# Single tiles of a gather fetched row by row: from SyncE alone to SyncE and ScalarE

## The chip, the cores and the metric

The kernel runs on one core of one Trainium2 chip. Times are device microseconds of that core. One execution was also taken by the hardware profiler; its time and its trace are what the profile below shows. The engines are called PE (TensorE), DVE (VectorE), ACT (ScalarE), POOL (GpSimd) and SP (SyncE).

## The reference

A graph layer with attention over all edges. There are 12500 nodes with 64 features and 412500 edges, sorted by receiver (`dst`), with 32 features each.

```
h   = relu(layernorm(x))
msg_in     = [h[src], h[dst], edge]                      # 64 + 64 + 32 per edge
messages   = silu(msg_in @ W1 + b1) @ W2 + b2
att_logits = silu(msg_in @ Wa1 + ba1) @ Wa2 + ba2
att        = softmax(att_logits, over all edges)
aggregated = segment_sum(messages * att, dst)            # per node
out = x + silu([h, aggregated] @ Wu1 + bu1) @ Wu2 + bu2
```

## The kernel before

First, per node, two tables are computed and stored in memory: `ts_d` (what a sender contributes to `msg_in @ [Wa1, W1]`, 128 floats, 512 bytes a row) and `tr_d` (the same for a receiver, with the bias). Then `one_pass` goes over the edges.

Edges come in tiles of 128 (one edge per partition), T = 3224 tiles; K = 8 tiles make a group, so there are NG = 403 groups. For each group the kernel needs the 128 x 8 sender rows. `load(g)` gets them: for each tile GpSimd issues one indirect DMA (line 487) that gathers 128 rows of `ts_d` into `gs`, a buffer from a pool of eight. The receivers of a group are few and lie close together, so their rows come as a window: SyncE loads it with two DMAs (line 506, `wins`, three buffers), and every fourth group it loads edge features and receiver numbers (lines 496 and 499, `eo` and `db`). DVE makes a one-hot matrix from the receiver numbers (line 513), and PE multiplies it and the edge features with the window (line 517) into `pe`.

`begin(g)` adds `pe` to the gathered rows (line 523) and ACT takes the tanh of it (line 526). `end(g)` makes messages and logits on DVE (lines 536 to 547). Groups are put in batches of four for a running softmax: two Exp on ACT (lines 575 and 578) once per batch. `by_node` and the parts of `sum_up` weigh the messages, sum them by node on PE (line 594), copy the sum on ACT (`out_of`, line 600), project it (line 605) and add it to the node sums on DVE (lines 618 to 624).

The main loop is software-pipelined: at iteration g it runs `begin(g)`, then `load(g + 2)`, then `end(g)`, with the summing of an older group in between. Compute instructions are pinned to the order in which they are written. DMAs, register loads and indirect DMAs are not pinned: the scheduler places them on their engine's queue, in the order of its own model, and each engine then runs its queue strictly in order. Every DMA of SyncE and ScalarE counts on one of eight semaphores, given out in turn, and waits until the DMA that had the same semaphore before has landed.

In some groups one tile of the eight is not gathered by GpSimd. This is the subject here. `QUEUES` lists who fetches such single tiles: `(engine, every, phase, n_rows)`. Before, it holds one entry: SyncE, one group in 11, 12 rows in each group. `numbers(q, g)` loads the 128 sender numbers of the tile into `one_src` (line 438). Then `rows(q, g)`, called once per group, loads the next 12 numbers into registers (line 460, one register load from memory) and issues 12 DMAs of one row of 512 bytes each (line 464) into the tile `one_gs`, kept in `alone`. After 11 groups all 128 rows are issued, the group's `load` then gathers 7 tiles only, and `begin` adds the single tile by an instruction of its own (line 525). SyncE's `rows` is called in `load`, behind the window's DMAs.

Of the kernel before, what the change touches and what calls it, by code (L numbers as in the profile page):

```python
# [49 lines left out]
ENG = mybir.EngineType  # L50
# [19 lines left out]
NC = 8  # L70
TABLES = 4

QUEUES = [(ENG.SP, 11, 0, 12)]
EPS = 1e-5
NEG = -3.0e38
BIG = 3.0e38
# [9 lines left out]
def gnn_kernel(ctx: ExitStack, tc: tile.TileContext, n_edges, x, src, src_row, dst, dst_row, first, edge,  # L86
# [70 lines left out]
    with tc.tile_pool(name="node1", bufs=1) as node1, \  # L157
# [132 lines left out]
        for c, nn in chunks:  # L290
            tr = node.tile([P, CB, C], F32, name="tr")[:, :nn, :]
            for b in range(0, nn, 4):
                n = min(4, nn - b)
                pn = node_ps.tile([P, 4, C], F32, name="pn", bufs=4)
                for i in range(0, n, 2):
# [7 lines left out]
        pin(nc.scalar.dma_start(hT_d, hT))  # L303

    one_pass(tc, n_edges, locals())
    again = nc.values_load(wrong[0:1, 0:1], min_val=0, max_val=1,
                           skip_runtime_bounds_check_because="it is the outcome of a comparison")
# [57 lines left out]
def one_pass(tc, n_edges, v):  # L365
# [17 lines left out]
    with ExitStack() as ctx:  # L383
# [25 lines left out]
        for w in wins:  # L409
            nc.vector.memset(w, 0.0)  # L410
            for r in range(2):
                rows = slice(WR + r * DE, WR + (r + 1) * DE)
                nc.vector.tensor_copy(w[rows, :, r, :], we[rows, None, :].to_broadcast([DE, 2, C]))
        with tc.tile_pool(name="work2", bufs=2) as work2, \
# [18 lines left out]
            def numbers(q, g):  # L433

                if g < NG - 4:
                    t = g * K + K - 1
                    rows_at[q, g] = small.tile([1, P], I32, name=f"one_src{q}", bufs=2)
                    nc.sync.dma_start(rows_at[q, g], v["src_row"][:, t * P:(t + 1) * P])

            def rows(q, g):  # L440
                engine, every, phase, n_rows = QUEUES[q]
                if g == 0:
                    numbers(q, phase + every)
                if g < phase:
                    return
                at = (g - phase) % every
                g = g - at + every
                if at == 0:
                    rows_at.pop((q, g - every), None)
                    if (q, g) in rows_at:  # L450
                        alone[g] = work2.tile([P, C], F32, name=f"one_gs{q}")
                if at == every // 2:
                    numbers(q, g + every)
                if (q, g) not in rows_at:
                    return
                a = at * n_rows
                n = min(n_rows, P - a)
                if n <= 0:
                    return
                load, regs = nc.values_load_multi_w_load_instructions(  # L460
                    rows_at[q, g][0:1, a:a + n], engines=[engine], min_val=0, max_val=NP - 1,
                    skip_runtime_bounds_check_because=WHY)
                for k in range(n):
                    dma[engine].dma_start(alone[g][a + k:a + k + 1, :], ts_d[bass.ds(regs[k], 1), :])
# [15 lines left out]
            def load(g):  # L480
# [24 lines left out]
                for r in range(2):  # L505
                    nc.sync.dma_start(win[r * R:(r + 1) * R, :, r, :],
                                      tr_w[bass.ds(at_sp[g], R), :, :])
                for q in range(len(QUEUES)):
                    if QUEUES[q][0] == ENG.SP:
                        rows(q, g)  # L510
# [9 lines left out]
            def begin(g):  # L520

                n = K - (g in alone)
                pin(nc.vector.tensor_tensor(gss[g][:, :n, :], pes[g][:, :n, :], gss[g][:, :n, :], ALU.add))  # L523
                if n < K:
                    pin(nc.vector.tensor_tensor(gss[g][:, n, :], pes[g][:, n, :], alone.pop(g), ALU.add))
                pin(nc.scalar.activation(pes[g], gss[g], AF.Tanh))  # L526

            def end(g):

                s = batch[g]  # L530
                if g == starts[s]:
                    lgs[s] = small.tile([P, B * K], F32, name="lg")
                gs, th = gss.pop(g), pes.pop(g)

                def message():
                    pin(nc.vector.scalar_tensor_tensor(acts[g % ACTS][:, :, 0:U], th[:, :, U:C], 1.0,  # L536
                                                       gs[:, :, U:C], op0=ALU.add, op1=ALU.mult))

                if g < NG - 1:
                    message()  # L540
                att = th[:, :, 0:U]
                pin(nc.vector.scalar_tensor_tensor(att, th[:, :, 0:U], 1.0, gs[:, :, 0:U],  # L542
                                                   op0=ALU.add, op1=ALU.mult))
                pin(nc.vector.tensor_tensor(att, att, wa2[:, None, :].to_broadcast([P, K, U]),  # L544
                                            ALU.mult))
                k = (g - starts[s]) * K
                pin(nc.vector.tensor_reduce(lgs[s][:, k:k + K], att, AX.X, ALU.add))  # L547
                if g == starts[s] + size[s] - 1:
                    mts[s] = top(s)
                if g == NG - 1:  # L550
                    message()
# [108 lines left out]
            for g in range(NG):  # L660
# [3 lines left out]
                if more and g == NG - 1:  # L664
                    next(more)
                begin(g)
                if more and g < NG - 1:
                    next(more)
# [368 lines left out]
```

## Time and profile before

| what | value |
|---|---|
| median of 2 runs | 6256.53 us (6245.09 to 6267.97) |
| the profiled execution's own time | 4115.52 us |
| its span, first to last instruction | 4113.8 us |
| mean granted TensorE clock in it | 0.633 |
| gathers by GpSimd (line 487) | 3188, 3018.7 us busy |
| rows by SyncE (line 464) | 4608 of 0.5 KB |
| mean busy share of the DMA engines, 1000 to 4050 us | 0.36 to 0.38 |
| waits of ACT before the tanh (line 526) | 2585.7 us |

The span and the engine shares belong to the profiled execution, which took less than the two timed ones. Busy time does not hold register, branch, semaphore and DMA-issuing instructions. So SyncE and the issuing part of ScalarE have no share in the page's first part; they are seen in the timeline as "SPq" and "ACTq". A group's line gives busy time, the mean duration in ns, and behind the bar the idle time of the engine before such instructions with what ended most of it. "issue" there means that the engine waited for nothing that the profile shows.

### The profile page before, as it was taken

Reading aid. Unit: us, or ns where it says so; the run is one execution under the profiler, and the core shown is the slowest. Engines: PE = TensorE matmul, PEld = TensorE weight load, DVE = VectorE, ACT = ScalarE, POOL = GpSimd, SP = SyncE. Lnnn points to the kernel's source line nnn. Section 1 sums busy time; section 2 is a strip of 40 time slices with the busy share of each in tenths; the row PEclk is TensorE's granted clock in tenths of the full one; section 3 lists DMA queues with packets and bytes.
Section 4 is the critical chain, followed back from the end, with each engine's and each line's share of the span. In section 5 each row is a group of like instructions: output and inputs, shape, how many; then the busy total and the mean of one; then the engine's idle time right before and its main releaser. Section 6 shows DMA issues by size and latency. Waiting matters only on the chain.

```text
span 4113.8 us, 59789 instructions
## 1 busy us (share of the span) xinstructions
PE 2284.8 (56%) x10980; PEld 1852.9 (45%) x10980; DVE 3021.4 (73%) x8518; ACT 584.3 (14%) x1235; POOL 3035.8 (74%) x3213
## 2 busy tenths in 40 slices
PE   5555545555556555556555555555555555555555
PEld 4444434444445444444444444444444444444444
DVE  6777867777777777777777777777777777777777
ACT  3211111111111111111111111111111111111112
POOL 3777777777777777777777777777777777777773
PEclk8666666666565666665566666666666556566665
DMA  7344443443434333333333333333333333333334
GB/s 270 88 102 101 99 105 92 105 101 97 102 93 99 86 91 84 88 91 81 91 84 89 91 81 91 83 89 91 81 91 82 91 91 81 92 81 90 91 78 112
DMA packets 220602, 393.50 MB, mean 96 GB/s; under 512 B 77077, under 2 KB 146554, under 8 KB 207034
## 3 DMA queue, kind: packets, MB, share of 16 engines
q0 software_dynamic: 102016, 209.13, 20.8%
q1 hardware_dynamic: 116826, 170.81, 17.0%
q10 hardware_dynamic: 1376, 9.67, 0.6%
q14 instruction: 294, 2.41, 0.2%
q8 instruction: 90, 1.47, 0.2%
HBM read 363.58 MB, written 25.72 MB: 95 GB/s over the span
## 4 chain that ended last, share of the span: by engine, by line


## 5 line engine op out<-in xcount | busy, mean ns | idle before, releaser
L487 POOL DMA_INDIRECT gs<-ts_d,src_sb x3188 | 3018.7, 947 | 1022.1 <-issue 952.1
L517 PE MATMUL pe<-wins,eo 128*128 128x256 f32 x3224 | 1477.3, 638 | 967.7 <-DVE eo L513 819.6
L517 PEld LDWEIGHTS pe<-wins,eo 128*128 128x128 f32 x3224 | 1000.5, 325 | 1265.8 <-DVE eo L513 970.2
L523 DVE TENSOR_TENSOR gs<-pe,gs 128x1024 f32<-128x1024 f32 (+1 forms) x403 | 487.7, 1211 | 775.5 <-DMA gs<-ts_d,src_sb 740.0
L526 ACT ACTIVATE pe<-gs 128x1024 f32<-128x1024 f32 x403 | 413.8, 1027 | 2585.7 <-DVE gs L523 1997.7
L588 DVE TENSOR_SCALAR wt<-iota_w,dloc,p 128x40 f32<-128x40 f32 x3224 | 734.0, 320 | 0.1
L594 PE MATMUL sp<-wt,acts 128*65 128x40 f32 x6448 | 608.9, 267 | 0.7 <-DVE wt L588 0.7
L594 PEld LDWEIGHTS sp<-wt,acts 128*65 128x65 f32 x6448 | 578.7, 183 | 1.0 <-DVE wt L588 0.8
L605 PEld LDWEIGHTS mt<-ss,w2u 65*128 65x128 f32 x806 | 224.8, 293 | 371.3 <-issue 321.5
L513 DVE TENSOR_SCALAR eo<-db,bj 64x256 f32<-64x256 int32 x806 | 259.7, 360 | 158.6 <-DMA db<-in_dst_row_dram 151.5
L564 PE MATMUL mt<-ident,mx 128*128 128x128 f32 x103 | 45.1, 437 | 547.3 <-DVE sums L622 538.2
L605 PE MATMUL mt<-ss,w2u 65*128 65x40 f32 x806 | 184.9, 324 | 261.4 <-DVE gm L571 257.9
L542 DVE SCALAR_TENSOR_TENSOR pe<-pe,gs 128x512 f32<-128x512 f32 x403 | 281.3, 698 | 13.0
L544 DVE TENSOR_TENSOR pe<-pe,w_all 128x512 f32<-128x512 f32 x403 | 281.4, 698 | 12.8
L536 DVE SCALAR_TENSOR_TENSOR acts<-pe,gs 128x512 f32<-128x512 f32 x403 | 278.2, 690 | 15.7 <-ACT pe L526 4.0
L547 DVE TENSOR_REDUCE lg<-pe 128x8 f32<-128x512 f32 x403 | 278.4, 691 | 13.7
L564 PEld LDWEIGHTS mt<-ident,mx 128*128 128x128 f32 x103 | 18.4, 179 | 557.7 <-issue 556.0
L624 DVE COPY stand<-nmax 64x40 f32 x806 | 163.4, 203 | 0.6
L622 DVE TENSOR_TENSOR sums<-sums,mt 64x40 f32 x600 | 113.2, 189 | 15.0 <-PE mt L605 10.9
L575 ACT ACTIVATE scale<-fall 128x1 f32<-128x1 f32 x103 | 20.9, 203 | 645.1 <-DVE fall L574 629.2
L600 ACT COPY ss<-sp 65x40 f32<-65x40 f32 x403 | 73.5, 182 | 20.7 <-PE sp L594 20.3
L618 DVE SCALAR_TENSOR_TENSOR sums<-sums,scale,mt 64x40 f32 x206 | 51.6, 251 | 11.4 <-PE mt L605 7.3
(92 smaller groups left out, 577.7 us busy)
## 6 DMA issues: line engine op xcount, KB each, us to landing
one_gs<-ts_d SPq DMA_DIRECT2D x4608, 0.5 KB
eo<-in_edge_dram SPq DMA_DIRECT2D x100, 512.0 KB
db<-in_dst_row_dram SPq DMA_DIRECT2D x200, 256.0 KB
gs<-ts_d,src_sb POOLq DMA_INDIRECT x3188
wins<-tr_d SPq DMA_DIRECT2D x806, 32.0 KB
ts_d<-ts SPq DMA_DIRECT2D x5, 896.0 KB
tr_d<-tr ACTq DMA_DIRECT2D x5, 896.0 KB
hT_d<-hT ACTq DMA_DIRECT2D x1, 3136.0 KB
```

The lines of the kernel that those rows point to most:

```text
L487: nc.gpsimd.indirect_dma_start(out=gs[:, j, :], out_offset=None, in_=ts_d[:, :], in_offset=bass.IndirectOffsetOnAxis(ap=src_sb[:, t + j:t ...
L513: pin(nc.vector.tensor_scalar(eo[:WR, e], db[:, e], bj[:, g, h:h + 1], None, op0=ALU.is_equal))
L517: pin(nc.tensor.matmul(pe[:, 2 * q:2 * q + 2, :], eo[:, q * P:(q + 1) * P], win[:, q // 2, :, :], start=True, stop=True))
L523: pin(nc.vector.tensor_tensor(gss[g][:, :n, :], pes[g][:, :n, :], gss[g][:, :n, :], ALU.add))
L526: pin(nc.scalar.activation(pes[g], gss[g], AF.Tanh))
L536: pin(nc.vector.scalar_tensor_tensor(acts[g % ACTS][:, :, 0:U], th[:, :, U:C], 1.0, gs[:, :, U:C], op0=ALU.add, op1=ALU.mult))
L542: pin(nc.vector.scalar_tensor_tensor(att, th[:, :, 0:U], 1.0, gs[:, :, 0:U], op0=ALU.add, op1=ALU.mult))
L544: pin(nc.vector.tensor_tensor(att, att, wa2[:, None, :].to_broadcast([P, K, U]), ALU.mult))
L547: pin(nc.vector.tensor_reduce(lgs[s][:, k:k + K], att, AX.X, ALU.add))
L588: pin(nc.vector.tensor_scalar(wt[:, j, :], iota_w[:, j // H, :], dloc[:, g * K + j:g * K + j + 1], p[:, k + j:k + j + 1], op0=ALU.is_equal ...
L594: pin(nc.tensor.matmul(sp, acts[g % ACTS][:, j, :], wt[:, j, :], start=j == 0, stop=j == K - 1))
L605: pin(nc.tensor.matmul(pp, w2u.rearrange("s h u -> s (h u)"), sps.pop(g), start=True, stop=True))
```

## The change

There are now two entries in `QUEUES`. SyncE fetches a single tile for one group in twelve, 12 rows per group. ScalarE fetches one for one group in sixteen, starting two groups later, 8 rows per group; its rows are issued by a call in `begin`, written behind the tanh. The row numbers of both are loaded by SyncE.

```diff
-QUEUES = [(ENG.SP, 11, 0, 12)]
+QUEUES = [(ENG.SP, 12, 0, 12), (ENG.Activation, 16, 2, 8)]
@@ in begin(g)
                 if n < K:
                     pin(nc.vector.tensor_tensor(gss[g][:, n, :], pes[g][:, n, :], alone.pop(g), ALU.add))
                 pin(nc.scalar.activation(pes[g], gss[g], AF.Tanh))
+                for q in range(len(QUEUES)):
+                    if QUEUES[q][0] == ENG.Activation:
+                        rows(q, g)
```

The functions that this uses are unchanged:

```python
def rows(q, g):
    engine, every, phase, n_rows = QUEUES[q]
    ...
    at = (g - phase) % every
    g = g - at + every          # the group whose single tile is being fetched
    ...
    a = at * n_rows
    n = min(n_rows, P - a)
    ...
    load, regs = nc.values_load_multi_w_load_instructions(
        rows_at[q, g][0:1, a:a + n], engines=[engine], ...)
    for k in range(n):
        dma[engine].dma_start(alone[g][a + k:a + k + 1, :], ts_d[bass.ds(regs[k], 1), :])
```

## The prediction

> **What bounds the kernel now.** I read the page first: engine shares, then the costliest groups. Columns of the first line are busy time, share of the span and instruction count; of the group lines, count, busy us and mean ns, then the idle time before the group and what ended it.
>
> ```profile
> span 4113.8 us, 59789 instructions
> PE 2284.8 (56%) x10980; PEld 1852.9 (45%) x10980; DVE 3021.4 (73%) x8518; ACT 584.3 (14%) x1235; POOL 3035.8 (74%) x3213
> ...
> L487 POOL DMA_INDIRECT gs<-ts_d,src_sb x3188 | 3018.7, 947 | 1022.1 <-issue 952.1
> ...
> L523 DVE TENSOR_TENSOR gs<-pe,gs 128x1024 f32<-128x1024 f32 (+1 forms) x403 | 487.7, 1211 | 775.5 <-DMA gs<-ts_d,src_sb 740.0
> L526 ACT ACTIVATE pe<-gs 128x1024 f32<-128x1024 f32 x403 | 413.8, 1027 | 2585.7 <-DVE gs L523 1997.7
> ```
>
> VectorE (73%) and GpSimd (74%) look equal, but their idle time differs. VectorE waits for something real, 740 us for gathers. GpSimd's idle ended on "issue": it waited for nothing. So a gather costs its 947 ns plus a gap that always follows it. The timeline, second and third columns start and length, shows this beat, with what SyncE and ScalarE do beside it:
>
> ```profile
> 2014.12 0.86 SPq L506 DMA_DIRECT2D wins<-tr_d  x2
> 2014.21 0.94 POOL L487 DMA_INDIRECT gs<-ts_d,src_sb  x1 [0.30 <-issue]
> ...
> 2015.46 0.94 POOL L487 DMA_INDIRECT gs<-ts_d,src_sb  x1 [0.30 <-issue]
> ...
> 2015.91 1.22 DVE L523 TENSOR_TENSOR gs<-pe,gs 128x1024 f32<-128x1024 f32 x1 [0.21 <-issue]
> ...
> 2016.15 4.82 SPq L464 DMA_DIRECT2D one_gs<-ts_d  x12
> 2016.71 0.94 POOL L487 DMA_INDIRECT gs<-ts_d,src_sb  x1 [0.30 <-issue]
> ...
> 2017.17 1.03 ACT L526 ACTIVATE pe<-gs 128x1024 f32<-128x1024 f32 x1 [0.93 <-DVE gs L523]
> ```
>
> Gathers start every 1.25 us (2014.21, 2015.46, 2016.71), whatever VectorE does. GpSimd's whole timeline runs so from 50.42 to 4042.24: 3188 gathers x 1.25 = 3985 us of those 3992. The group beat is 8 x 1.25 = 10.0 us. VectorE needs 3021.4/403 = 7.5 us a group, PE 5.7. The waits of SyncE's queue tell that it too has room; its long waits are for buffers that PE frees:
>
> ```profile
> SPq L506 <- PE pe L517: 291.7, 69, 9.9
> SPq L506 <- PE mt L605: 256.1, 138, 10.8
> SPq L506 <- PE sp L594: 99.0, 84, 5.2
> ```
>
> So in the profiled execution GpSimd's count of gathers sets the time. The chain section is empty and cannot confirm it.
>
> The profiled execution took 4115.52 us (span plus 1.7), the median of the two runs shown is 6256.53: 2141 us more, a factor of 1.520. No view shows where these lie. A step may carry over unchanged, or stretched by 1.520; I keep both ends.
>
> **What the Trainium skill says.** "DMA: Bandwidth & Descriptors", section "Issuing engines are not separate DMA queues": DMAs from different engines run on the same 16 DMA engines, and several issuers save only issue time. That is the question here: rows are issued beside GpSimd, and it is GpSimd's issue time that binds. The DMA engines have room, mean share 0.36 to 0.40 in the windows of the loop. The section "Latency and other measured facts" of that page gives a register load from memory a floor of about 600 ns; the trace has 527 at least and a median of 933 ns for line 460, and I use the trace. "SBUF — State Buffer", section "SBUF: two separate sides", warns that VectorE in its two-port modes keeps GpSimd from writing descriptors. The trace disagrees for this execution: gathers last 940 to 944 ns from minimum to median. In the longer runs it could be what adds time, which no view decides; then a gather costs more and removing one saves more.
>
> **The change part by part.**
>
> Singles before: one in 11 groups, 11 to 396, makes 36 (4608 rows / 128). After: SyncE's groups 12 to 396 step 12 are 33, ScalarE's 18 to 386 step 16 are 24; 12a = 16b + 2 has no solution, so none coincide. 57 singles: 21 gathers fewer, 3167, and the changed program's order holds 3167.
>
> Gathers: 21 x 1.25 = -26.2 us, all on the path. Stretched by 1.520: -39.9.
>
> SyncE: 33 x 128 = 4224 rows, 384 fewer. A burst of 12 takes 4.82 us, 0.40 each: -154 us; 33 x 11 = 363 instead of 396 register loads, -33 x 0.93 = -31 us; 21 more loads of row numbers, x 0.29 (10.4 us busy over 36 in the trace) = +6. About -180 us, off the path: SyncE waits for PE anyway. Counted 0.
>
> ScalarE: 24 x 128 = 3072 issues and 24 x 16 = 384 register loads. ScalarE issued only big DMAs in the trace, so a row's cost there is not shown. The nearest row is SyncE's 0.40 us: 3072 x 0.40 + 384 x 0.93 = 1229 + 357 = 1586 us, or 8 x 0.40 + 0.93 = 4.1 us in a group. Beside its 584 us that is 53% of the span. It lies in the 2585.7 us that ScalarE idles before line 526. Tanh takes 1.03 us, starts right after the add and leaves 10.0 - 1.1 = 8.9 us; the row work fits twice. Low bound 0; high bound: its cover gone, what exceeds 8.9 us in a group goes to VectorE. Taken: 0.
>
> How late may tanh be? In the timeline the add at 2008.05 ends at 2009.28, tanh at 2010.34, and the first user (line 536) starts at 2012.23: 1.9 us free. Beyond it VectorE has 10.0 - 7.5 = 2.5 us a group. Behind those stand eight gather buffers, so that GpSimd may run several groups ahead while VectorE catches up. This matters because the rows aren't spread evenly. In the changed program's order 173 of 403 intervals between tanhs hold none, and about 30 hold 24 to 33. Thirty-two rows are 32 x 0.40 + 4 x 0.93 = 16.5 us, 7.6 over the 8.9. VectorE regains that in three groups at 2.5. Counted 0.
>
> VectorE: 21 groups more split the add, 128 x 128 apart in 0.28 us (36 x 272 to 281 ns), while the rest of the add shrinks by an eighth. Under 21 x 0.28 = 6 us, beside waits for gathers. 0.
>
> DMAs: a row moved to ScalarE or left with a gather moves the same 512 bytes. 0.
>
> Sum: 4115.5 - 26.2 = 4089.3 us against the profiled execution. Onto the median: 6256.5 - 26.2 = 6230.3 unchanged, 6256.5 - 39.9 = 6216.6 stretched. I take the middle, 6223 us, -0.5%.
>
> **The rivals.**
>
> Slower: the two queues lock each other. In both programs every DMA of SyncE or ScalarE waits for the landing of the one eight places earlier, over eight semaphores that both queues now share in turn. Of 3072 ScalarE rows, 1301 wait on a DMA of SyncE; 1000 SyncE rows and 210 window loads (line 506) wait on a row of ScalarE. ScalarE stands at tanh until the add; SyncE can then go no more than eight DMAs further, and the window for the matmul of line 517 stands behind. If SyncE thereby loses its lead and works only after tanh, a group is: 1.25 add + 1.03 tanh + SyncE's 11 rows x 0.40 = 4.4, register load 0.93, two windows 0.87, a quarter of eo and db (1.5/4 = 0.4) + two landings across queues. A landing is about 1.5 us after issue for window loads (median 1.47 from the trace's landing records). Sum 11.9 us. It decides from 10.0 on: 1.9 x 384 groups = +730 us at most. I put half of it in the rival, since SyncE keeps some lead in the intervals without rows: +365 us. The rival's time: 6256.5 - 26 + 365 = 6595 us. For it: the waits and the bunching are in the order. Against: SyncE's own work falls by 180 us, and buffers give all sides groups of lead. With all of it, 6960.
>
> Faster: SyncE sets the pace of the longer runs. Less the 122 us before the first and after the last gather their group beat would be 6135/403 = 15.2 us, with about 15 DMAs of SyncE, 1.0 us each. Taking 384 of about 5900 away (section 6 of the page, summed) gives -6.5%, 6135 x 0.065 = 399: 5858 us. For it: the unexplained 2141 us. Against: 0.40 us a row in the trace, and SyncE's waits for PE.
>
> No gain: the gathers go, but VectorE or the late tanhs eat the 26 us: 6256 us.
>
> That the change doesn't do what it says is excluded by the 3167 gathers in the order.
>
> **How the numbers follow.** Forecast 0.55, no gain 0.07, locked queues 0.28, SyncE's relief 0.10. Two per cent is 125 us, about what a measurement of this kernel can tell from no change. Forecast and no gain lie within it, and 0.01 of the locked case where it is mild: same 0.63, slower 0.27, faster 0.10. Own range of the forecast: 6170 to 6280 (two-run spread of 0.4% around 6217 to 6230). The range must add 0.2 from the sides: up over the mild and middle locked cases to 6600, down to 6120, which leaves out the relief and the worst lock.
>
> **What would show it.** Right: gathers still every 1.25 us, 3167 of them, ending near 4016 instead of 4042; span near 4088; line 464 on ScalarE at 0.4 us a row; VectorE's waits before line 523 still for gathers. Locked queues: gaps over 0.30 us before gathers, waits of VectorE at line 536 on tanh or of PE at line 517 on wins, and SyncE's waits on PE gone over to its row DMAs. Wrong altogether: a span unchanged while the timed runs move by over 2%; then what binds those is not in the profile.

## The result and the profile after

The change made the kernel slower: 6480.8 us against 6256.5 us (two runs each), ratio 1.038 (1.034 to 1.042). One thing must be known to read any number here: the kernel before takes 6245 to 6394 us on some chips and 4114 to 4123 us on others, and by its time its profile above is of the second kind, while the result is of the first. Ratios below are always to the kernel before on the same chip.

The page of the changed kernel, engine shares and groups:

```profile
span 6482.8 us, 68399 instructions
PE 2277.8 (35%) x10980; PEld 1859.6 (29%) x10980; DVE 3011.0 (46%) x8539; ACT 608.5 (9%) x1235; POOL 3012.3 (46%) x3192
...
L487 POOL DMA_INDIRECT gs<-ts_d,src_sb x3167 | 2995.1, 946 | 3357.4 <-issue 3213.6
L517 PE MATMUL pe<-wins,eo 128*128 128x256 f32 x3224 | 1457.7, 631 | 3228.3 <-DMA wins<-tr_d 1762.1
...
L526 ACT ACTIVATE pe<-gs 128x1024 f32<-128x1024 f32 x403 | 413.7, 1027 | 1384.5 <-DMA one_gs<-ts_d 504.0
```

The gathers are the 3167 foreseen and last 946 ns as before, but GpSimd now idles 3357 us, although the line still says "issue". It does wait: GpSimd's semaphore instructions ahead of the gathers last 10.1 us at the median, where all took at most 43 ns in the kernel before. (Three numbers are the shortest, median and longest duration in ns; first the changed kernel, then the kernel before from its profile above.)

```profile
L487 POOLq EVENT_SEMAPHORE  x399: 17/10132/32252, 47.1 to 6341.2; - x200
```

```profile
L487 POOLq EVENT_SEMAPHORE  x399: 17/43/43, 47.3 to 4026.2; - x200
```

All engines are busy under half of the time. A lower clock is not the reason: the mean granted one fell from 0.633 to 0.589, but PE's busy time is 2277.8 us against 2284.8. Nor are slower transfers: by section 3 of the pages the packets of the gathers took 12.9% of 6482.8 us, 836 us, against 20.8% of 4113.8 us, 856 us. The longest wait of PE's matmuls has become the window of receiver rows (1762 us, `wins`), a DMA of SyncE. So look at SyncE's instructions, in the same two profiles:

```profile
L464 SPq MOVE one_gs<-ts_d x4224: 2/29/1409, 140.8 to 6330.4; - x192
...
L464 ACTq MOVE one_gs<-ts_d x3072: 2/29/1395, 132.7 to 6010.4; - x192
```

```profile
L464 SPq MOVE one_gs<-ts_d x4608: 29/29/38, 89.5 to 3937.1; - x192
```

A move into a register, 29 ns at the median, lasts up to 1409 ns. Instruction by instruction the trace shows spells, mostly of 5 to 25 us, in which each instruction of SyncE, whatever it is, comes about 0.70 us after the one before (or 1.40). Counted from the instruction records, such spells fill some 2700 to 3300 of the 6483 us; the sum depends on how the pauses inside a spell are counted. The profile on which the prediction rests has no slow move at all. A piece of the timeline shows what one does:

```profile
2004.93 15.08 SPq L464 DMA_DIRECT2D one_gs<-ts_d  x8
...
2008.96 0.62 PE L608 MATMUL mt<-ss,w2u 65*128 65x40 f32 x2 [6.59 <-DVE gm L574]
...
2009.38 1.96 PE L597 MATMUL sp<-wt,acts 128*65 128x40 f32 x16
...
2019.84 0.19 DVE L625 TENSOR_TENSOR sums<-sums,mt 64x40 f32 x1 [9.20 <-remote]
...
2020.06 0.19 ACT L603 COPY ss<-sp 65x40 f32<-65x40 f32 x1 [10.31 <-remote]
...
2020.26 0.86 SPq L506 DMA_DIRECT2D wins<-tr_d  x2
...
2025.10 0.94 POOL L487 DMA_INDIRECT gs<-ts_d,src_sb  x1 [7.49 <-issue]
```

Eight rows take SyncE 15.08 us, 1.9 us each instead of 0.40, and the window load behind the rows goes out only at 2020.26. A second thing is late. DVE's addition of line 625 and ScalarE's copy of line 603 need what PE's matmuls of lines 608 and 597 made, which by the trace were over at 2009.58 and 2011.34; both start at 2020. "remote" says that a semaphore rose just before, but that no instruction which raises it had just ended. The semaphore is PE's: it is recorded to rise at 2007.76 and then at 2019.82. So the signal that PE is done comes some 10 us late, in the same spell. GpSimd uses up its buffers and stops 7.49 us. Lastly, the waits of SyncE's queue, in us, number and longest:

```profile
SPq L464 <- DMA one_gs<-ts_d: 190.3, 214, 7.6
SPq L506 <- DMA one_gs<-ts_d: 169.1, 50, 13.9
SPq L499 <- DMA one_gs<-ts_d: 119.9, 42, 6.0
```

SyncE now waits 479 us for rows to land, through the semaphores that the two queues share. Its waits for PE, which led this list before, are nearly gone in the loop: it has lost its lead.

### The profile page after: what moved, and what is told of

Read it like the earlier page. It is cut to its first block, busy times and chain, and to the rows that moved or that the text cites. A ratio compares the mean times of both kernels' runs of the same rounds, so it can differ in the third digit from the quotient of the medians.

```text
span 6482.8 us, 68399 instructions
## 1 busy us (share of the span) xinstructions
PE 2277.8 (35%) x10980; PEld 1859.6 (29%) x10980; DVE 3011.0 (46%) x8539; ACT 608.5 (9%) x1235; POOL 3012.3 (46%) x3192
## 3 DMA queue, kind: packets, MB, share of 16 engines
q0 software_dynamic: 101344, 207.76, 12.9%
## 4 chain that ended last, share of the span: by engine, by line
## 5 line engine op out<-in xcount | busy, mean ns | idle before, releaser
L517 PE MATMUL pe<-wins,eo 128*128 128x256 f32 x3224 | 1457.7, 631 | 3228.3 <-DMA wins<-tr_d 1762.1
L591 DVE TENSOR_SCALAR wt<-iota_w,dloc,p 128x40 f32<-128x40 f32 x3224 | 715.4, 307 | 0.1
L574 DVE TENSOR_REDUCE gm<-mt 128x1 f32<-128x128 f32 x103 | 29.2, 284 | 401.6 <-remote 401.5
```

The costliest lines, as they stand in the source:

```text
L517: pin(nc.tensor.matmul(pe[:, 2 * q:2 * q + 2, :], eo[:, q * P:(q + 1) * P], win[:, q // 2, :, :], start=True, stop=True))
L591: pin(nc.vector.tensor_scalar(wt[:, j, :], iota_w[:, j // H, :], dloc[:, g * K + j:g * K + j + 1], p[:, k + j:k + j + 1], op0=ALU.is_equal ...
```

## The experiments

My theory after the result (the "starved queue"): on some chips SyncE and ScalarE run slowly in spells, and time goes with what stands on their queues. Its rival, from the record: the two queues lock each other by the shared semaphores.

### The kernel before, and each part of the change alone

The kernel before, with its trace:

> The kernel before, unchanged, with its trace. Starved queue (my new theory): in the profile of the changed kernel SyncE has spells in which each of its instructions, even a register move that else takes 29 ns, lasts 0.70 us; they fill about 3285 of 6483 us. The profiled execution of before had none and took 4115 us. If the two timed runs of before (6245 and 6268 us) had them, this trace shows them for about 2900 to 3200 us, gathers interrupted, and a time near 6256. Locked queues (the rival on record): no such spells here, since only SyncE issues rows; a time near 4115, or 6256 with another cause.

No single tiles:

```diff
-QUEUES = [(ENG.SP, 12, 0, 12), (ENG.Activation, 16, 2, 8)]
+QUEUES = []
```

> No single tiles at all: all 3224 tiles are gathered by GpSimd, SyncE issues some 1300 DMAs instead of 5900. Starved queue: SyncE has about 13,800 instructions fewer (three for each of 4608 rows), spells vanish or shrink to a few per cent, GpSimd binds again: 122 + 3224 x 1.25 = 4150 us, ratio 0.66 to the 6256 us of before. If GpSimd's gathers bound the timed runs at 1.9 us each (my prediction's stretched case): 36 more gathers, about 6325 us, ratio 1.01. Locked queues: 4150 to 6325, it says nothing on this one.

SyncE's part alone:

```diff
-QUEUES = [(ENG.SP, 12, 0, 12), (ENG.Activation, 16, 2, 8)]
+QUEUES = [(ENG.SP, 12, 0, 12)]
```

> SyncE's part of the change alone: one group in twelve on SyncE, nothing on ScalarE; 3191 gathers, 4224 rows. Starved queue: SyncE has 384 x 3 + 33 instructions fewer of 17,900, 6.6%; ratio about 0.94 to before, 5880 us. GpSimd bound, stretched: +3 gathers x 1.9 = 6 us, ratio 1.00. Locked queues: as before, 1.00, the loss is then all in ScalarE's part.

ScalarE's part alone:

```diff
-QUEUES = [(ENG.SP, 12, 0, 12), (ENG.Activation, 16, 2, 8)]
+QUEUES = [(ENG.Activation, 16, 2, 8)]
+                if engine == ENG.Activation:
+                    for one in load if isinstance(load, (list, tuple)) else [load]:
+                        pin(one)
                 for k in range(n):
-                    dma[engine].dma_start(...)
+                    row = dma[engine].dma_start(...)
+                    if engine == ENG.Activation:
+                        pin(row)
```

> ScalarE's part of the change alone: one group in sixteen on ScalarE, 8 rows a group, none on SyncE, with ScalarE's row DMAs and register loads kept in written order behind the tanh; 3200 gathers, 3072 rows. Starved queue: if the spells come with the number of instructions of a queue, ScalarE now has 9,600 more and would have spells, but fewer than SyncE had: 4400 to 5400 us, ratio 0.70 to 0.86. If they come with SyncE only: 4120 us, 0.66. Locked queues: SyncE has few DMAs left, so little to lock: near 1.00 of before or what GpSimd allows.

| kernel (kernel before 6394 us) | gathers | rows by SyncE, by ScalarE | us | ratio (95%) |
|---|---|---|---|---|
| before again | 3188 | 4608, 0 | 6404 (one run) | - |
| no single tiles | 3224 | 0, 0 | 5718 | 0.894 (0.891 to 0.897) |
| SyncE's part | 3191 | 4224, 0 | 6219 | 0.973 (0.969 to 0.977) |
| ScalarE's part | 3200 | 0, 3072 | 5810 | 0.909 (0.905 to 0.912) |

The first trace settles where the 2141 us that I could not place lie. The kernel before at 6402 us has the spells, and the profiled execution at 4114 us has not:

```profile
span 6402.2 us, 59789 instructions
...
L464 SPq MOVE one_gs<-ts_d x4608: 2/29/1410, 148.6 to 6258.8; - x192
```

On such a chip a row is not cheap but dear: with 36 more gathers the kernel without rows is 10.6% faster than the one before, where GpSimd's count would make it slower. The size I expected, 4150 us, was missed: spells remain. Without rows SyncE has 3618 instructions left, and now others stand still:

```profile
ACT ss L603 <- remote: 2777.1, 158, 24.2
PEld mt L608 <- ACT ss L603: 2169.8, 115, 23.1
```

ScalarE's short copy (line 603) waits up to 24.2 us, and PE waits for it. It is again PE's signal that is late. In this trace 135 of the 403 copies start more than 3 us after the last matmul of line 597 before them had ended, with ScalarE idle, and in 130 of these a rise of PE's semaphore is recorded in the 0.15 us before the start; the first profile of the kernel before has no such copy. So the spells don't only slow instructions on a queue, as my theory says: signals between engines come late too. SyncE's part alone gives 0.973 where 0.94 was expected of the number of instructions. ScalarE's alone is a miss: 5810 us, where 4400 to 5400 (0.70 to 0.86) was expected. Nor does the time simply go with the number of rows: on this chip the first 384 rows taken from SyncE gave 175 us, the other 4224 only 500 us.

When do the spells come? From the four traces of that chip I took GpSimd's runs of gathers (starts under 2.5 us apart) and the register instructions of SyncE. In the kernel before 1594 of them lasted over 600 ns. 1379 lie inside a run, most of them after its first 5 us, and the other 215 within 6 us after its end. Later than 6 us after a run there are over 3200 register instructions of normal length (under 60 ns) and no slow one; in a run's first 5 us 241 are slow and 2252 normal, between 10 and 20 us 611 and 211. So the spells go with uninterrupted gathering and end soon after GpSimd pauses. GpSimd pauses when its eight buffers are full, and they are emptied by the engines that the spell holds up. That is a correlation in the traces; what starves the queues is not shown. Uninterrupted gathering alone doesn't do it: in the first profile of the kernel before all 3188 gathers are one such run, without a slow register instruction.

### Rows from fixed addresses, and fewer gather buffers

Two experiments were to change the spells: the same DMAs with fewer instructions, and shorter runs of gathers.

```diff
-                    dma[engine].dma_start(alone[g][a + k:a + k + 1, :], ts_d[bass.ds(regs[k], 1), :])
+                    dma[engine].dma_start(alone[g][a + k:a + k + 1, :], ts_d[a + k:a + k + 1, :])
```

> The kernel before with the row DMAs reading fixed rows instead of those named by registers: the same 4608 DMAs of 512 bytes, but the register load and the two register instructions ahead of each DMA are gone. It leaves out the right choice of rows. Starved queue, by instructions: SyncE loses 9600 of its 17,900 instructions, two thirds of what the rows cost (676 us over the kernel without rows): near 5940 us, ratio 0.93. By DMAs: the rows cost what they did, ratio 1.00.

```diff
-    gather = ctx.enter_context(tc.tile_pool(name="gather", bufs=8))
+    gather = ctx.enter_context(tc.tile_pool(name="gather", bufs=4))      # none_b4; 3 in none_b3
```

> No single tiles and four gather buffers instead of eight, so that GpSimd can run ahead by less. In the traces all slow register instructions of SyncE lie in runs of gathers without a break or within 4 us after one, nearly all after its first 5 us; without single tiles a run is 24 gathers at the median, and GpSimd then pauses for a buffer. If the run length drives the spells: shorter runs, fewer stalls, faster than the kernel without single tiles, 5000 to 5500 us. If GpSimd's lead hides the stalls: fewer buffers expose them, slower than 5718.

> The same with three gather buffers, the fewest that the order of the loop allows. A run can hardly pass 8 to 16 gathers. If the run length drives the spells: at or under the time with four buffers. If the lead hides the stalls, or gathers are now exposed behind the end of a group (10 us of gathers + 2 us of landing against three groups): slower, 5900 or more.

Beside them ran the changed kernel with ScalarE's rows in written order (the edit of ScalarE's part, with both entries of `QUEUES`):

> The changed kernel with ScalarE's register loads and row DMAs kept in written order, so that 8 rows stand behind each tanh instead of 0 to 33. Starved queues alone (spells of slow instructions while gathers run, each part costing by itself): the parts measured so far add up, none + 500 us for SyncE's rows + 92 us for ScalarE's = 6310 us, ratio 0.987 to before. Locked queues (shared semaphores tie the two queues, worse where rows are bunched): SyncE still waits hundreds of us for ScalarE's rows; if the bunching makes the lock, 0.99; if the sharing itself makes it, 1.02 to 1.04 as the changed kernel.

They ran on a chip without spells, kernel before 4114 us. Fixed rows 1.0005 (0.9996 to 1.0013): SyncE has 8684 instructions instead of 17,902, and that is worth nothing there. Four buffers without single tiles 1.013 (1.011 to 1.015), three 1.025 (1.023 to 1.026). Rows in written order 0.998 (0.998 to 0.999). What they were meant to tell of the spells they cannot.

### The changed kernel on a chip without spells

> The changed kernel again, beside the kernel before on the same chip. The chips differ: on one the kernel before took 6394 us with spells of slow instructions, on another 4114 us without. Without spells: GpSimd bound says 4114 - 26 = 4088 us, ratio 0.994; locked queues with bunched rows say slower than the version with rows in written order (4107 us, 0.998), 4115 to 4600, ratio 1.00 to 1.12. With spells: 1.038 as measured.

> The changed kernel with ScalarE's rows in written order, 8 behind each tanh, again. Without spells: 0.998 as measured. With spells: if bunching makes the loss, the parts add up, 0.987; if the shared semaphores do, whatever the order, 1.02 to 1.04.

> The kernel before with rows from fixed addresses (it leaves out the right choice of rows), 9600 instructions of SyncE fewer, the same DMAs. Without spells 1.0005 as measured. With spells: if they cost by instructions, 0.93; if by DMAs, 1.00.

> No single tiles and four gather buffers. Without spells 1.013 as measured (eight buffers would give 3224 gathers x 1.25 = 1.009). With spells: if the length of GpSimd's runs drives them, under 0.894, what eight buffers gave; if the lead hides the stalls, over it.

Kernel before 4115 us. Changed kernel 1.013 (1.011 to 1.015), with rows in written order 0.9985 (0.998 to 0.999), fixed rows 1.000, four buffers without single tiles 1.0125. The four once more, on another chip:

> The changed kernel with ScalarE's rows in written order, beside the changed kernel. On a chip without spells 0.998 to 0.999 as measured twice. On a chip with spells: if bunching alone makes the loss, the parts measured there add up, 0.987; if the shared semaphores make it in any order, as the changed kernel, 1.02 to 1.04.

> The changed kernel again. Without spells 1.013 as measured; with spells 1.038 as measured.

> The kernel before with rows from fixed addresses (it leaves out the right choice of rows). Without spells 1.000. With spells: by instructions 0.93, by DMAs 1.00.

> No single tiles and four gather buffers. Without spells 1.013. With spells: under 0.894 if the length of GpSimd's runs drives them, over 0.894 if its lead hides the stalls.

This chip has no spells either (kernel before 4123 us): 0.998, 1.012, 1.000 and 1.013.

So the change loses even where no instruction is slow: +51 us where -26 was forecast. And it is the order of ScalarE's rows that makes the loss, since keeping them in written order takes it away. (The traces show what the order does: between two tanhs stand 8 rows in 382 of 402 cases; as scheduled, none in 173 and 24 to 33 in 27.) The windows of the trace show where. Columns: window, its length, busy us with counts for PE, PE's loads, DVE, ACT and GpSimd, then clock, DMA share and GB/s. First the kernel before, then the changed one, then the one in written order:

```profile
620.00:1320.00 700.00, 404.57 (x1932) 321.53 (x1931) 528.16 (x1508) 99.16 (x214) 529.89 (x559) 0.63 0.40 99
1320.00:2020.00 700.00, 385.17 (x1856) 314.32 (x1856) 511.27 (x1460) 90.49 (x196) 529.19 (x561) 0.62 0.37 88
```

```profile
620.00:1320.00 700.00, 360.61 (x1720) 281.54 (x1721) 474.38 (x1358) 92.85 (x194) 478.68 (x505) 0.62 0.36 91
1320.00:2020.00 700.00, 379.86 (x1941) 316.76 (x1941) 534.34 (x1532) 97.62 (x204) 528.12 (x559) 0.64 0.36 88
```

```profile
620.00:1320.00 700.00, 384.83 (x1802) 292.95 (x1802) 497.53 (x1427) 98.82 (x204) 522.56 (x552) 0.63 0.39 97
```

Behind 1320 us GpSimd issues 559 gathers in 700 us, its full beat. Between 620 and 1320 it is 505: 54 fewer than before, x 1.25 = 67 us. All its nine gaps of over 3 us lie there, and on the next chip nine lie at the same places. In written order the stretch costs 7 gathers, 9 us.

The stretch is only where the loss becomes visible. The starts of the tanhs show where it arises (us later than the tanh of the same group in the kernel before):

| group | 16 | 55 | 120 | 130 | 402 |
|---|---|---|---|---|---|
| the changed kernel | 22 | 50 | 101 | 105 | 42 |
| rows in written order | 5 | 14 | 46 | 51 | -16 |

Up to 660 us, just before group 55, GpSimd loses nothing, since its eight buffers take up the lag: at 660 us it has gathered 7 groups ahead of the tanh, in the kernel before 1. From there on further lag shows as gaps of GpSimd. The lag grows mainly in groups 16 to 120 (some 260 to 1360 us), in which SyncE also carries the node biases and the rest of the inputs (lines 320, 342, 357, 362) and ScalarE copies them (line 339). One of the gaps, in the changed kernel's timeline:

```profile
737.92 5.45 SPq L464 DMA_DIRECT2D one_gs<-ts_d  x7
...
740.87 0.19 ACT L603 COPY ss<-sp 65x40 f32<-65x40 f32 x1 [5.63 <-PE sp L597]
741.02 5.61 ACTq L464 DMA_DIRECT2D one_gs<-ts_d  x11
...
743.43 1.25 SPq L320 DMA_DIRECT2D hb<-hT_d  x2
...
748.95 0.58 ACT L339 COPY bu<-mt 64x512 f32<-64x512 f32 x1 [7.89 <-PE mt L322]
...
749.55 1.12 SPq L342 DMA_DIRECT2D bq_d<-bu  x2
...
751.23 0.33 SPq L499 DMA_DIRECT2D db<-in_dst_row_dram  x1
...
755.17 0.61 DVE L513 TENSOR_SCALAR eo<-db,bj 64x256 f32<-64x256 int32 x2 [13.19 <-DMA db<-in_dst_row_dram]
...
759.55 0.94 POOL L487 DMA_INDIRECT gs<-ts_d,src_sb  x1 [8.39 <-issue]
```

ScalarE's copy of line 603 waits 5.63 us for PE, and its rows stand behind it, from 741.02. SyncE needs 5.45 us for seven rows (0.78 each), since it waits for one of those rows to land: in the instruction records one of its rows goes out at 739.92 and the next at 742.74, after a wait of 2.4 us. The loads of `hb` stand behind (743.43). PE works on them, ScalarE copies at 748.95, the two stores of `bq_d` wait for that copy, and the second `db` load stands behind the stores (751.23). DVE waits 13.19 us for it, and GpSimd is out of buffers for 8.39 us. The stores stand ahead of that `db` load in the kernel before too (12 times, in the changed kernel 8 times), and there no gap of over 3 us follows; new is that a row of ScalarE behind an unready copy delays what comes after it. This is the lock. It is read off the trace and not tested by itself: before seven of the nine gaps SyncE waits for rows of ScalarE, 1.6 to 5.5 us in the 16 us ahead, before the other two (of 5.1 us each) it does not. And the waits alone are not the loss. In the three longest entries of its list SyncE waits for rows 688 us in this trace and still 636 us in written order, where the loss is gone. What shrinks there is the lag, to half. A late tanh as such is excluded: VectorE waits 21.9 us for it in all, 0.3 us in the stretch.

### ScalarE's rows behind that stretch

```diff
-QUEUES = [(ENG.SP, 12, 0, 12), (ENG.Activation, 16, 2, 8)]
+QUEUES = [(ENG.SP, 12, 0, 12), (ENG.Activation, 16, 130, 8)]
```

> The changed kernel with ScalarE's first fetch at group 130 instead of 2, that is, behind the stretch (groups 16 to 120, some 620 to 1320 us) in which SyncE also moves the node biases and the rest of the inputs: 3175 gathers. In the trace of the changed kernel without spells all of GpSimd's gaps of over 3 us lie in that stretch, 67 us more than before. If that collision is the loss: 4114 - 13 x 1.25 = 4098 us, ratio 0.996. If the locked queues cost everywhere: half to all of the loss stays, 1.005 to 1.012. With spells: 1.02 to 1.04 if the lock costs there everywhere.

> The same with ScalarE's rows in written order. Without spells: 4098 us, 0.996, if the 23 us that GpSimd still lost in gaps of the pinned version (9 before) came from the same stretch; 0.998 as the pinned version if not. With spells: 0.99 if bunching made the loss, 1.02 to 1.04 if the shared semaphores do.

These two ran on a chip with spells, kernel before 6245 us: 1.026 (1.021 to 1.031) as scheduled and 1.024 (1.017 to 1.031) in written order. So the test of the stretch itself is not made. (Groups 16 to 120, which the expectation puts at 620 to 1320 us, run from some 260 to 1360 us.) But they tell something of the spells. SyncE's waits for rows, first as scheduled, then in written order:

```profile
SPq L506 <- DMA one_gs<-ts_d: 149.6, 38, 15.3
SPq L464 <- DMA one_gs<-ts_d: 149.2, 199, 8.3
SPq L499 <- DMA one_gs<-ts_d: 110.4, 38, 6.5
```

```profile
SPq L467 <- DMA one_gs<-ts_d: 78.0, 83, 5.4
...
SPq L511 <- DMA one_gs<-ts_d: 23.9, 13, 3.1
SPq L504 <- DMA one_gs<-ts_d: 12.8, 4, 5.0
```

They fall from 409 to 115 us, and the time stays within the intervals. On such a chip neither bunching nor SyncE's waits for rows set the loss. ScalarE's spells grow instead: of its 4098 register instructions 139 last over 0.6 us as scheduled, 617 in written order. The sharing of semaphores as such is not excluded, since ScalarE's rows use them in both orders.

## Why the prediction was wrong

*GpSimd sets the time at 1.25 us a gather.* Right for the profiled execution and, in the kernel before, for chips without spells; the spacing is 1.25 us at the median on both kinds (1.249 to 1.252), also in the changed kernel. On chips with spells it is not the bound; GpSimd is busy 46%.

*Carrying the sum over to the median.* This is the step that failed. I had 2141 us that no view showed, and put them into one factor: the gain unchanged, or stretched by 1.520, -26 to -40 us. That assumed that the missing time is more of the same. It was another regime, in which instructions and signals are late and a row costs more than the gather that it saves: there the kernel without any single tile takes 0.894 of the time, and the change measured +224 us. Both ends of my interval came from one sign. The rival in which SyncE sets the pace had the right engine, but I gave it 0.10 and let it speak for a gain, since I only counted the 384 rows that leave SyncE. That part exists: SyncE's part alone is 0.973 (that rival's 5858 us would be 0.936). With the rows of ScalarE added to it the kernel has 1.038, though measured on another chip.

*ScalarE's 1586 us of row work counted 0.* The cost of a row was right: without spells ScalarE's rows go out 0.38 us apart at the median. Its place was wrong. On the chip with spells its rows alone cost 0.909 - 0.894 = 0.015 over no rows. The parts' excesses over no rows, 0.079 and 0.015, would sum to a ratio of 0.987, 6310 us on that chip; the changed kernel had 1.038, 6481 us, on another chip of that kind. So some loss seems to come only when both queues carry rows, 5% by the ratios, 170 us by the times. Its size is uncertain, since the kernel before differs by 149 us between chips with spells. ScalarE's rows were in written order in that part and not in the change, but the late versions (1.026 and 1.024) agree in both orders.

*"VectorE regains that in three groups", and SyncE "off the path", both counted 0.* This is the second step that failed, by itself, on chips without spells. VectorE's spare time of 2.5 us a group says nothing of how fast the whole chain catches up, in which SyncE's loads and ScalarE's copies take part: from group 130 to the end the lag falls from 105 to 42 us, 0.23 us a group. And a page-wide average of 7.5 us a group hides groups 16 to 120, in which SyncE and ScalarE carry more. The terms of 0 measured 67 us of gathers, and -26 + 67 = +41 is what the last gather shows, 4084.0 us against 4042.2. The profiled execution ends 45 us later than that of before; the medians differ by 51.

*The locked queues.* Without spells the order of ScalarE's rows is shown to make the loss (1.013 to 0.9985), and the lock is seen at work in most of the gaps. I priced it at 365 us in all groups; it was 67 us, visible in one stretch. The measured 6481 us lies near the rival's 6595, but that is luck: on such a chip the lock is not shown to be the cause.

*The Trainium skill's "SBUF — State Buffer"*, section "SBUF: two separate sides", was named for VectorE keeping GpSimd from writing descriptors, as a possible source of the missing time by gathers that take longer. The trace excludes that source: gathers last 938, 945 and 1387 ns (shortest, median, longest) on a chip with spells. It doesn't contradict the page, since no run here shows whether an operation of VectorE was in one of the modes of which the page speaks.

Open: what delays instructions and signals, and why on some chips only (four chips ran these experiments, two of each kind, and each was of one kind in all its runs); whether recording the executions has a part in it; whether a row costs there by its instructions or by its DMA (fixed rows had no run there); whether fewer gather buffers help there; and whether, and by which link, rows on both queues are dearer than their sum.

No version beats both kernels on both kinds of chips. With spells it is the one without single tiles (0.894), without spells the change in written order (0.9985); four buffers without single tiles cost 1.3% there. What single tiles are worth there with eight buffers was not run; an estimate from 36 gathers of 1.25 us is 45 us, 1.1%.

## What to carry to other kernels

When a profiled execution and the timed ones differ by half, as here, suspect that the profile is of another regime: don't scale a sum onto the median, name what could bind instead, and keep both signs in the range. Work put on an idle engine's queue also enters every order that this queue shares with others, here eight semaphores and the tanh that all wait for; keep such DMAs in written, even order (worth 1.4% here, on chips without spells). Before counting a lag as regained, look for stretches with extra work, and follow one instruction of each group through two traces: buffers hide a lag until they are full.

## What the runs showed of the hardware

The same program took 4114 us on one chip and 6394 us on another. The difference goes with spells, mostly of 5 to 25 us, in which SyncE passes one instruction in about 0.70 us (or 1.40), 29 ns register moves included, while GpSimd gathers without pause; gathers themselves keep their 1.25 us. Register moves of ScalarE take up to 1395 ns in such spells, and PE's semaphore was seen to rise some 10 us after the matmuls had ended (2009.58 and 2019.82 us in the changed kernel).
